# Tying each indirect DMA of two expert layers to a preceding matmul, and dealing the DMAs out in another rhythm

## The chip, the cores and the metric

The kernel runs on one NeuronCore of one Trainium2 chip. The metric is the device time of one execution in microseconds, and the time of a version is the median of several executions. Five engines run side by side, each in its own program order: TensorE (PE in the profile; its weight loads are shown apart as PEld), VectorE (DVE), ScalarE (ACT), GpSimd (POOL) and SyncE (SP, which here only issues DMAs). They wait for one another through semaphores.

## The reference

The program is a chain of eight blocks on an activation `x` of 8 sequences by 512 tokens by 128 channels, all in float32. What follows is cut to the order of the blocks and to the expert layer, which the change concerns.

```python
x = x + circulant_ssm(layernorm(x))       # "rotate" block
x = x + ffn(layernorm(x))                 # "lora" block
x = x + encoder(layernorm(x))             # 4 layers of linear attention
x = x + ffn(layernorm(x))
x = x + rotary_attention(layernorm(x))    # "attended" steps
x = x + experts(layernorm(x))             # expert layer m
x = x + gated_linear_attention(layernorm(x))   # "gated" steps
x = x + experts(layernorm(x))             # expert layer n, then the output

def experts(x):                           # 8 experts, the best 2 for each token
    xn = rms_norm(x, norm_scale)
    scores = einsum('bsd,ed->bse', xn, w_router)
    ids = top_k(scores, 2)[1]
    c = take_along_axis(softmax(scores), ids, -1)
    val, gate = split(einsum('bsd,ehd->bseh', xn, w_up), 2, -1)   # hidden size 352
    y = einsum('bseh,edh->bsed', val * silu(gate), w_down)
    return x + sum(take_along_axis(y, ids[..., None], 2) * c[..., None], 2)
```

## The kernel before, in words

**Experts by sorting.** Class `Experts` does one expert layer, here called m (the first) and n (the second). Its sequences are cut into groups: m has two groups of 4 sequences, n has three groups of 2, 4 and 2. For one group the work goes like this.

1. `choose` (VectorE, with four small matmuls) finds the two best experts of each token and, from counts, a slot for each (token, expert) pair, so that slots of one expert lie in whole tiles of 128. It is a generator of twelve steps, and the last one fills the list `todo`.
2. `posts` issues the indirect DMAs on POOL's queue. A **row** (line 1122, `slots<-xn,rpos`) scatters 128 tokens to their slots in DRAM. There are 2 for every 128 tokens, that is 32 rows for a group of 4 sequences and 16 for a group of 2.
3. `tiles` is a generator that does one expert tile of 128 slots in each turn. `fetch` reads four tiles of slots back (line 1168, `xr<-slots`, on SP's queue); it waits for **all** rows of the group. `turned` transposes them (line 1179). Then each tile has two matmuls of width 352 (lines 1235 and 1236), ACT's tanh (1241), two VectorE operations (1248 and 1249), three transposes (1199), a copy by ACT (1201), six matmuls (1208) and ACT's copy to `yr` (1211). A group of 4 sequences has 39 tiles, a group of 2 has 23. The steps are pipelined over turns: a turn does the first matmuls of tile i, the transposes of i-1 and the last matmuls of i-2.
4. For each finished tile, `posts` issues a **given** (line 1133, `given<-yr,to`): an indirect DMA that scatters 128 results to where their tokens are.
5. `combine` reads the results back (line 1267, after all givens of the group) and adds them to `x` (line 1285).

`posts` is a generator as well. Each call of `next` issues at most one DMA: a row if `todo` has one and fewer than 5 finished tiles are waiting, else a given. If nothing is ready it does nothing.

**Order.** The context manager `in_program_order` makes each of PE, DVE, ACT and POOL run its instructions in the order in which the Python code emits them, with one freedom (rows of one group among themselves). So the time at which a DMA can be issued depends on what stands before it in POOL's order, among which are the rsqrt operations that the norms need (line 165 for `ln_rs` and `g_rs`, 966 for `m_rs`, 1663 for `g_rn`). The places of all this are set by hand:

- In `attended_and_experts`, `pipeline` runs the attention's steps for the 8 sequences. Near its end the side stream `first` is called once after every step: `choose` of m's group one, then its rows. Whatever is left of `first` runs after it.
- Then `blend` deals three streams over 42 turns: the tiles of m's group one, `choose` of group two, and `posts`.
- In `gated_and_experts`, `pipeline` runs the gated steps for 4 pairs of sequences, with a side stream `dealt` that has numbered places: `at(now, i)` is place i of round `now`, and each round has 29 places. `before` is layer m, `posts` its remaining DMAs, `own` the DMAs of layer n, and `tiles` the turns of layer n. The gated steps fall in rounds -1 to 4; round 5 holds only tiles, DMAs and `choose`.
- A second `blend` deals the turns of layer n that are left, with `own` and with `combine` of its first two groups. What is left of `own` and the last group's `combine` follow.

Of the kernel before, what the change touches and what calls it, by code (L numbers as in the profile page):

```python
# [912 lines left out]
class Experts:  # L913
# [24 lines left out]
    def apart(self, rows, made):  # L938
# [7 lines left out]
        self.loose[made.ins.name] = group  # L946
        rows.append(made.ins)

    def steps(self, b):

        k, nc = self.k, self.k.nc
# [158 lines left out]
        self.todo.extend((g, t, i) for t in range(g.n) for i in range(2))  # L1110
        yield

    def posts(self, many, upto=0):

        nc = self.k.nc
        while many and not (upto and all(len(g.back) == g.tiles for g in self.groups[:upto])):
            given = [g for g in self.groups if g.ready]
            if self.todo and sum(len(g.ready) for g in given) < 5:  # L1120
                g, t, i = self.todo.pop(0)
                made = nc.gpsimd.indirect_dma_start(  # L1122
                    out=g.slots,
                    out_offset=bass.IndirectOffsetOnAxis(ap=g.pos[:, i, t : t + 1], axis=0),
                    in_=g.xn[:, t, :],
                    in_offset=None,
                )
                self.apart(g.rows, made)
                many -= 1
            elif given:  # L1130
                g = given[0]
                yr, to = g.ready.pop(0)
                made = nc.gpsimd.indirect_dma_start(  # L1133
                    out=g.given,
                    out_offset=bass.IndirectOffsetOnAxis(ap=to, axis=0),
                    in_=yr,
                    in_offset=None,
                )
                self.apart(g.back, made)
                many -= 1  # L1140
            yield

# [149 lines left out]
def chain(*streams):  # L1292
    for one in streams:
        yield from one
# [4 lines left out]
        pass  # L1299


def slow(stream, idle):

    for _ in stream:
        for _ in range(idle + 1):
            yield


def fast(stream, many):

    while True:
        for _ in range(many):
            if next(stream, stream) is stream:
                return
        yield


def idle(many):
    yield from range(many)
# [54 lines left out]
def attended_and_experts(k, o, slots, keep, work, banks, close):  # L1374

    tc = k.tc
    with tc.tile_pool(name="moe1", bufs=1, side="right") as room:
        m = Experts(k, "m", slots, keep, room)  # L1380
        one, two = m.groups
        with tc.tile_pool(name="cau2", bufs=2) as pool, k.banks(**banks["after"]):
            after = attended_steps(k, o, pool)

            def steps(b):
                yield from after(b)
                yield from m.steps(b)

            with in_program_order(tc, m.loose):
                first = chain(m.choose(one), slow(m.posts(2 * one.n), 1))  # L1390


                pipeline(
                    steps,
                    B,
                    (0, 1, -1, 2, 3, -2, 1, -1, 0, 3, 2, 0, 3, 4),
                    side=first,
                    every=1,
                    first=one.seqs + 4,
                )  # L1400
                run(first)
        close()
        m.p3 = work()
        m.hidden()
        with k.banks(**banks["experts"]), in_program_order(tc, m.loose):
            n = turns(one)
            posts = m.posts(2 * two.n + one.tiles + two.tiles)
            blend((m.tiles(one), n), (fast(m.choose(two), 2), n), (chain(idle(3), take(fast(posts, 2), n - 3)), n))
    return m, posts


def gated_and_experts(k, before, posts, slots, keep, banks, out):
# [3 lines left out]
    with tc.tile_pool(name="moe1", bufs=1, side="right") as room:  # L1416
# [5 lines left out]
        with tc.tile_pool(name="gla1", bufs=1) as alone, tc.tile_pool(name="gla", bufs=2) as pool:  # L1422
            with k.banks(**banks["gated"]):
# [15 lines left out]
                def at(now, *places):  # L1439
                    return [(now + 1) * len(ages) + i for i in places]  # L1440

                side = dealt(
                    (before.tiles(last), at(-1, *range(16), *range(17, 28, 2)) + at(0, *range(0, 29, 2)) + at(1, *range(5))),
                    (posts, at(-1, *range(29)) + at(0, *range(29)) + at(1, *range(6))),
                    (whole(posts), at(1, 6)),
                    (before.combine(first), at(-1, *range(6, 15))),
                    (before.combine(last), at(1, *range(8, 15), 17, 19)),
                    (m.choose(one), at(2, *range(19, 29)) + at(3, *range(3))),
                    (own, at(3, *range(3, 29)) + at(4, *range(29)) + at(5, *range(32))),
                    (own, at(5, *range(16, 32))),  # L1450
                    (tiles, at(3, *range(20, 29, 2)) + at(4, *range(0, 29, 4)) + at(5, *range(0, 30, 6))),
                    (m.choose(two), at(4, *range(19, 29)) + at(5, *range(3))),
                    (m.choose(three), at(5, *range(19, 32))),
                )
                with in_program_order(tc, before.loose, m.loose):
                    pipeline(steps, B // 2, ages, side=side, every=1)
                    run(side)
        with k.banks(**banks["experts"]), in_program_order(tc, m.loose):
            left = pieces - 18

            def combined(g):
                yield from until(lambda: len(g.back) == g.tiles)
                yield from idle(3)
                yield from m.combine(g)

            blend((tiles, left), (take(fast(own, 2), left), left), (chain(*(combined(g) for g in m.groups[:2])), left))
            run(own)
            run(m.combine(three))

# [864 lines left out]
```

## Time and profile before

| what | value |
|---|---|
| median of 3 runs | 2083.75 us (2075.97 to 2087.93) |
| profiled execution | 2091.69 us; span from its first to its last instruction 2090.0 us |
| busy, share of the span: PE, PEld, DVE, ACT, POOL | 83%, 57%, 60%, 45%, 35% |
| mean granted TensorE clock | 0.888 |
| rows issued | 128, of 974 ns each on POOL |
| givens issued | 163, of 968 ns each on POOL |
| DMA on POOL's queue | 20.47 MB, 2.9% of 16 engines' span |

In the profile, busy time is what an engine spends in its own instructions; issuing a DMA from SP isn't counted. "Idle before" is an engine's idle time ahead of an instruction, and the name after the arrow is what ended it: another engine's instruction, a DMA, "issue" when the profile shows no wait that ended just then, or "remote" when the semaphore was updated at that moment but no instruction of the profile ended close to it. The end of a matmul is computed by the profiler, not observed.

### The profile page before, as it was taken

Reading aid. Unit: us, or ns where it says so; the run is one execution under the profiler, and the core shown is the slowest. Engines: PE = TensorE matmul, PEld = TensorE weight load, DVE = VectorE, ACT = ScalarE, POOL = GpSimd, SP = SyncE. Lnnn points to the kernel's source line nnn. Section 1 sums busy time; section 2 is a strip of 40 time slices with the busy share of each in tenths; the row PEclk is TensorE's granted clock in tenths of the full one; section 3 lists DMA queues with packets and bytes.
Section 4 is the critical chain, followed back from the end, with each engine's and each line's share of the span. In section 5 each row is a group of like instructions: output and inputs, shape, how many; then the busy total and the mean of one; then the engine's idle time right before and its main releaser. Section 6 shows DMA issues by size and latency. Waiting matters only on the chain. (4 is left out here: it accounts for less than half of the span.)

```text
span 2090.0 us, 29883 instructions
## 1 busy us (share of the span) xinstructions
PE 1742.2 (83%) x10171; PEld 1189.5 (57%) x10171; DVE 1249.7 (60%) x4147; ACT 950.9 (45%) x1747; POOL 730.3 (35%) x866
## 2 busy tenths in 40 slices
PE   4998789999998698999988727898898886726995
PEld 2655567888776455444346515665565565614774
DVE  6654788888877654555546624456657844613554
ACT  1022556666654322666665413454545443403553
POOL 2111333333334421454454365522121114355342
PEclk9888899999998789999988858998999876857998
DMA  9600000000000200000000011221001001112232
GB/s 273 107 1 1 0 1 1 1 1 1 1 1 1 109 23 41 1 2 2 2 1 1 5 58 53 65 62 47 16 11 39 12 1 41 30 49 71 68 102 63
DMA packets 79390, 71.25 MB, mean 34 GB/s; under 512 B 6560, under 2 KB 73120, under 8 KB 78336
## 3 DMA queue, kind: packets, MB, share of 16 engines
q1 hardware_dynamic: 69120, 47.89, 8.9%
q0 software_dynamic: 9536, 20.47, 2.9%
q8 instruction: 86, 1.41, 0.3%
q10 hardware_dynamic: 576, 0.90, 0.1%
q14 instruction: 72, 0.59, 0.1%
HBM read 34.98 MB, written 34.25 MB: 33 GB/s over the span
## 5 line engine op out<-in xcount | busy, mean ns | idle before, releaser
L165 POOL TENSOR_TENSOR ln_rs<-rs_v,mhalf 128x4 f32<-128x4 f32 x144 | 150.9, 1049 | 427.3 <-DVE rs_v L164 412.8
L1133 POOL DMA_INDIRECT given<-yr,to x163 | 157.9, 968 | 339.5 <-ACT yr L1211 288.7
L1248 DVE SCALAR_TENSOR_TENSOR half<-half,ps_a 128x352 f32<-128x352 f32 x163 | 84.6, 519 | 243.5 <-ACT half L1241 205.9
L672 ACT ACTIVATE pr<-ps_s 128x1024 f32<-128x1024 f32 x160 | 155.1, 1021 | 64.6 <-PE ps_s L662 64.3
L1236 PE MATMUL ps_a<-w_m,xt 128*128 x326 | 136.0, 501 | 55.7 <-DVE half L1248 23.6
L1122 POOL DMA_INDIRECT slots<-xn,rpos x128 | 124.6, 974 | 61.5 <-issue 45.7
L676 POOL TENSOR_SCALAR_AFFINE_SELECT pr<-pr 128x256 f32<-128x256 f32 x256 | 101.4, 418 | 112.2 <-ACT pr L672 109.1
L1235 PE MATMUL ps_a<-w_m,xt 128*128 x326 | 135.7, 500 | 5.7 <-ACT xt L1181 4.1
L1201 ACT COPY gt<-ps_b 128x384 f32<-128x384 f32 x163 | 77.9, 478 | 131.3 <-PE ps_b L1199 99.4
L530 PEld LDWEIGHTS ps_c<-w_e,mlp_g 128*128 128x128 f32 x1024 | 126.6, 198 | 15.1 <-issue 14.8
L530 PE MATMUL ps_c<-w_e,mlp_g 128*128 128x128 f32 x1024 | 128.8, 281 | 0.1
L522 PE MATMUL ps_a<-zt,w_e 128*128 128x512 f32 x256 | 123.7, 607 | 0.9 <-ACT zt L211 0.9
L1236 PEld LDWEIGHTS ps_a<-w_m,xt 128*128 128x128 f32 x326 | 63.6, 203 | 104.7 <-DVE half L1248 33.8
L1241 ACT ACTIVATE half<-ps_a 128x352 f32<-128x352 f32 x163 | 75.5, 463 | 86.4 <-PE ps_a L1235 69.4
L178 DVE BATCH_NORM_AGGREGATE ln_mv<-ln_st 128x2 f32<-128x6 f32 x576 | 99.9, 178 | 16.0
L1199 PEld LDWEIGHTS ps_b<-w_ident,hid 128*128 128x128 f32 x489 | 64.7, 149 | 74.3 <-issue 34.6
L1199 PE MATMUL ps_b<-w_ident,hid 128*128 128x128 f32 x489 | 86.9, 289 | 20.2 <-DVE hid L1249 15.0
L1249 DVE SCALAR_TENSOR_TENSOR hid<-half,ps_a 128x352 f32<-128x352 f32 x163 | 85.0, 521 | 29.3 <-remote 7.5
L523 ACT ACTIVATE mlp_g<-ps_a,w_col 128x512 f32<-128x512 f32 x128 | 85.6, 686 | 35.4 <-PE ps_a L522 35.4
L224 POOL TENSOR_TENSOR xe<-xe,w_erow 128x512 f32<-128x512 f32 x64 | 82.2, 1304 | 55.2 <-DVE ks L480 52.8
L373 ACT ACTIVATE mlp_g<-ps_a,w_col 128x512 f32<-128x512 f32 x64 | 44.0, 687 | 125.5 <-PE ps_a L372 124.8
L662 PE MATMUL ps_s<-qm,rot 32*128 32x128 f32 (+3 forms) x1024 | 98.6, 472 | 2.1 <-ACT pr L672 2.1
(362 smaller groups left out, 4010.8 us busy)
## 6 DMA issues: line engine op xcount, KB each, us to landing
xr<-slots SPq DMA_DIRECT2D x37, 260.0 KB
y<-given SPq DMA_DIRECT2D x32, 256.0 KB
slots<-blank SPq DMA_DIRECT2D x3, 2535.0 KB
w_m<-in_m_dram SPq DMA_DIRECT2D x2, 2244.0 KB
w_e<-in_e_dram SPq DMA_DIRECT2D x2, 1700.0 KB
slots<-blank SPq DMA_DIRECT2D x2, 1495.0 KB
given<-yr,to POOLq DMA_INDIRECT x163
x<-in_u_dram SPq DMA_DIRECT2D x8, 256.0 KB
```

The source lines that it names most:

```text
L165: nc.gpsimd.tensor_tensor(out, v, self.mhalf[:, :n], ALU.pow)
L178: nc.vector.bn_aggr(mv[:, t, :], st[:, t, :])
L522: nc.tensor.matmul(ph, w1[:, c * P : (c + 1) * P], ht, start=True, stop=True)
L530: nc.tensor.matmul(py[:, t, :], g[:, c, t * P : (t + 1) * P], w2[:, c, :], start=(c == 0), stop=(c == 3))
L662: nc.tensor.matmul(halves[g // 2][:, g % 2, at : at + S - u * P], kr[rows, u * P : (u + 1) * P], qm[rows, i, u * P : S], start=True, stop= ...
L672: nc.scalar.activation(pr, sc, AF.Exp)
L676: nc.gpsimd.affine_select(out=v, in_=v, pattern=[[0, 2], [1, P]], compare_op=ALU.is_ge, fill=0.0, base=0, channel_multiplier=-1,)
L1122: made = nc.gpsimd.indirect_dma_start(out=g.slots, out_offset=bass.IndirectOffsetOnAxis(ap=g.pos[:, i, t : t + 1], axis=0), in_=g.xn[:, t, :],
L1133: made = nc.gpsimd.indirect_dma_start(out=g.given, out_offset=bass.IndirectOffsetOnAxis(ap=to, axis=0), in_=yr, in_offset=None,)
L1199: nc.tensor.transpose(pt[:, q, :], hid[:, q, :], k.ident)
L1235: nc.tensor.matmul(pg, xt, w["experts"][:, bass.ds(o + HID, HID)], start=True, stop=True)
L1236: nc.tensor.matmul(pv, xt, w["experts"][:, bass.ds(o, HID)], start=True, stop=True)
```

## The change

A method `behind` is added. After each indirect DMA is made, it looks back through the instructions emitted so far in the block, finds the last one of PE, and makes the DMA wait for it. The schedules by hand are changed as well: rows of m's group one come at every step instead of every second one; in the first `blend` the choice runs at three steps a turn and the DMAs at 2, 2 and 1, with what is left of group two's rows issued right after; in the gated rounds m's second group starts later, and n's DMAs, tiles and choice of group two are placed differently; in the last `blend` the DMAs come at 1 and 2 a turn instead of 2. The number of DMAs and all arithmetic stay as they were.

```diff
--- before.py
+++ after.py
@@ -946,6 +946,13 @@
         self.loose[made.ins.name] = group
         rows.append(made.ins)
 
+    def behind(self, made):
+        tc = self.k.tc
+        for i in reversed(tc.nc.cur_bb.bb.instructions):
+            if i.engine == mybir.EngineType.PE:
+                tc.add_manual_dep(made.ins, i.name, SYNC, reason="not all of them at once")
+                return
+
     def steps(self, b):
 
         k, nc = self.k, self.k.nc
@@ -1110,12 +1117,12 @@
         self.todo.extend((g, t, i) for t in range(g.n) for i in range(2))
         yield
 
-    def posts(self, many, upto=0):
+    def posts(self, many):
 
 
 
         nc = self.k.nc
-        while many and not (upto and all(len(g.back) == g.tiles for g in self.groups[:upto])):
+        while many:
             given = [g for g in self.groups if g.ready]
             if self.todo and sum(len(g.ready) for g in given) < 5:
                 g, t, i = self.todo.pop(0)
@@ -1126,6 +1133,7 @@
                     in_offset=None,
                 )
                 self.apart(g.rows, made)
+                self.behind(made)
                 many -= 1
             elif given:
                 g = given[0]
@@ -1137,6 +1145,7 @@
                     in_offset=None,
                 )
                 self.apart(g.back, made)
+                self.behind(made)
                 many -= 1
             yield
 
@@ -1299,20 +1308,14 @@
         pass
 
 
-def slow(stream, idle):
-
-    for _ in stream:
-        for _ in range(idle + 1):
-            yield
-
-
-def fast(stream, many):
+def fast(stream, *many):
 
     while True:
-        for _ in range(many):
-            if next(stream, stream) is stream:
-                return
-        yield
+        for n in many:
+            for _ in range(n):
+                if next(stream, stream) is stream:
+                    return
+            yield
 
 
 def idle(many):
@@ -1387,7 +1390,7 @@
                 yield from m.steps(b)
 
             with in_program_order(tc, m.loose):
-                first = chain(m.choose(one), slow(m.posts(2 * one.n), 1))
+                first = chain(m.choose(one), m.posts(2 * one.n))
 
 
                 pipeline(
@@ -1405,7 +1408,9 @@
         with k.banks(**banks["experts"]), in_program_order(tc, m.loose):
             n = turns(one)
             posts = m.posts(2 * two.n + one.tiles + two.tiles)
-            blend((m.tiles(one), n), (fast(m.choose(two), 2), n), (chain(idle(3), take(fast(posts, 2), n - 3)), n))
+            blend((m.tiles(one), n), (fast(m.choose(two), 3), n), (chain(idle(4), take(fast(posts, 2, 2, 1), n - 4)), n))
+            while len(two.rows) < 2 * two.n:
+                next(posts)
     return m, posts
 
 
@@ -1440,30 +1445,31 @@
                     return [(now + 1) * len(ages) + i for i in places]
 
                 side = dealt(
-                    (before.tiles(last), at(-1, *range(16), *range(17, 28, 2)) + at(0, *range(0, 29, 2)) + at(1, *range(5))),
+                    (before.tiles(last), at(-1, 4, *range(7, 29)) + at(0, *range(0, 29, 2)) + at(1, *range(4))),
                     (posts, at(-1, *range(29)) + at(0, *range(29)) + at(1, *range(6))),
+                    (posts, at(-1, *range(9))),
                     (whole(posts), at(1, 6)),
-                    (before.combine(first), at(-1, *range(6, 15))),
+                    (before.combine(first), at(-1, *range(9, 18))),
                     (before.combine(last), at(1, *range(8, 15), 17, 19)),
                     (m.choose(one), at(2, *range(19, 29)) + at(3, *range(3))),
                     (own, at(3, *range(3, 29)) + at(4, *range(29)) + at(5, *range(32))),
-                    (own, at(5, *range(16, 32))),
-                    (tiles, at(3, *range(20, 29, 2)) + at(4, *range(0, 29, 4)) + at(5, *range(0, 30, 6))),
-                    (m.choose(two), at(4, *range(19, 29)) + at(5, *range(3))),
+                    (own, at(5, *range(0, 32, 2))),
+                    (tiles, at(3, *range(20, 29, 2)) + at(4, *range(0, 29, 4)) + at(5, *range(0, 32, 4))),
+                    (fast(m.choose(two), 2), at(4, *range(19, 26))),
                     (m.choose(three), at(5, *range(19, 32))),
                 )
                 with in_program_order(tc, before.loose, m.loose):
                     pipeline(steps, B // 2, ages, side=side, every=1)
                     run(side)
         with k.banks(**banks["experts"]), in_program_order(tc, m.loose):
-            left = pieces - 18
+            left = pieces - 21
 
             def combined(g):
                 yield from until(lambda: len(g.back) == g.tiles)
                 yield from idle(3)
                 yield from m.combine(g)
 
-            blend((tiles, left), (take(fast(own, 2), left), left), (chain(*(combined(g) for g in m.groups[:2])), left))
+            blend((tiles, left), (take(fast(own, 1, 2), left), left), (chain(*(combined(g) for g in m.groups[:2])), left))
             run(own)
             run(m.combine(three))
 
```

## The prediction

> **What bounds the kernel now.** I first read the table by stage, PE against time, because the whole-span share (83% busy) mixes stages. Columns: stretch, length, busy time with instruction counts for PE, PEld, DVE, ACT and POOL, granted clock, DMA share, GB/s.
>
> ```profile
> core 0: us, PE busy (x) PEld busy (x) DVE busy (x) ACT busy (x) POOL busy (x), PEclk, DMA share, GB/s
> 1246.50:1355.00 108.50, 85.88 (x429) 60.90 (x430) 46.05 (x139) 40.87 (x104) 57.57 (x60) 0.86 0.20 60
> ...
> 1821.00:1915.00 94.00, 37.46 (x150) 26.32 (x150) 22.94 (x86) 14.05 (x36) 55.15 (x58) 0.63 0.16 49
> 1915.00:2071.00 156.00, 149.30 (x886) 114.99 (x885) 86.99 (x239) 85.56 (x206) 61.55 (x66) 0.99 0.27 80
> ```
>
> In the last stretch expert tiles run alone and PE is full: PE is the bound. Between 1821 and 1915 no compute engine is above 40%, and POOL is busiest, with indirect DMAs. Next I read the timelines of that dip, engine by engine: start, duration, instruction, and in brackets the idle time before it and its releaser.
>
> ```profile
> 1847.15 0.95 POOL L1122 DMA_INDIRECT slots<-xn,rpos  x1 [0.31 <-issue]
> 1848.41 0.96 POOL L1122 DMA_INDIRECT slots<-xn,rpos  x1 [0.30 <-issue]
> 1849.67 0.95 POOL L1122 DMA_INDIRECT slots<-xn,rpos  x1 [0.30 <-issue]
> ```
> ```profile
> 1843.26 1.54 PE L1236 MATMUL ps_a<-w_m,xt 128*128 x2 [6.68 <-issue]
> 1847.76 0.88 PE L1199 MATMUL ps_b<-w_ident,hid 128*128 128x128 f32 x3 [2.96 <-DVE hid L1249]
> 1869.17 1.65 PE L1208 MATMUL ps_a<-w_m,gt 128*128 x6 [20.53 <-ACT yr L1211]
> ```
> ```profile
> 1856.26 0.48 ACT L1201 COPY gt<-ps_b 128x384 f32<-128x384 f32 x1 [13.62 <-remote]
> 1868.85 0.27 ACT L1211 COPY yr<-ps_a 128x128 f32<-128x128 f32 x1 [12.11 <-remote]
> ```
>
> POOL issues a DMA every 1.26 us. The three transposes end at 1848.64, yet ACT's copy of them starts at 1856.26: 7.6 us late. It waits for PE's semaphore, whose update appears in the trace at 1856.19; four more updates of PE come within 0.2 us of one another, at 1868.8, after the burst has stopped. The work is done, and the message is late. So I counted, over the whole trace, PE instructions whose semaphore shows no update within 1 us of their end, by how many indirect DMAs POOL had just issued back to back (under 1.45 us apart): none, 1 of 1677; one, 3 of 312; two or three, 14 of 69; four to six, 26 of 58; seven or more, 15 of 17. **Runs of indirect DMAs delay other engines' semaphores**, and the delay begins at the third or so.
>
> The cost per stage comes from the starts of line 1235. A tile turn takes 2.19 us undisturbed, and 2.31 on average over n's group two (1919.6 to 2007.4, 38 gaps). m's group one takes 3.21 (1248.4 to 1370.4), and 2.87 in the part with one row and one given a turn (1285.2 to 1348.3, 22 gaps). In n's group one, one gap alone is 39.3 (1835.8 to 1875.1). Last, the waits of PE: before m's first tile it waits for the rows,
>
> ```profile
> PE ps_b L1179 <- DMA xr<-slots: 27.4, 2, 26.6
> ```
>
> and POOL's rows fill 1202.95 to 1241.97 there, broken only by one pair of rsqrts.
>
> **What the Trainium skill says.** "DMA: Bandwidth & Descriptors", section on SWDGE, HWDGE and iDMA: for a DMA issued from GpSimd its cores compute the descriptors and write them to rings in SBUF. The trace agrees that each occupies POOL, 0.96 us; that page says nothing of other engines' semaphores. "Perfetto Trace Analysis", section on the TensorE instruction: a matmul's end is estimated from its size, and the semaphore update comes after PSUM has acknowledged and must then propagate. That allows a gap; that 1676 of 1677 are under 1 us without a burst shows that 7.6 isn't the estimate's error. "TensorE: Matmul & The Clock Gate", section on what is happening: PE's clock falls to half after an idle window of about 3.4 us. The trace agrees: 0.50 in 1850 to 1880. A stall is thus paid for twice. The same page, section on the per-tile semaphore tail, prices an increment at 26.3 ns.
>
> **The change, part by part.** I count DMAs turn by turn from the streams.
>
> 1. *Waits.* 291 DMAs get one. Most of the matmuls named already signal; if all needed another increment, 291 x 26.3 ns = 7.7 us, an estimate from that page, spread over PE and mostly inside other engines' latency: 0 taken, 0 to 8 kept. On POOL a separate wait instruction exists before (at 1853.23), and the spacing there stays 1.26: 0. Queued behind a waiting DMA on POOL are the rsqrts; for them wait DVE's norms, then PE's transposes. Usually the rsqrt needs DVE results that need a later matmul than the one waited for. I take 0; the rival below has the other bound.
>
> 2. *Rows of m's group one.* POOL-bound: 32 x 1.26 = 40 us after `choose` ends at 1189. Before, POOL idled 5.8 us (1193.6 to 1199.4) for lack of rows in its order; doubling their rate fills that. But 14 rather than 7 rows now precede the last `m_rs` (8.8 us later), which the tail can bear, since PE waits for the rows anyway until 1246. The first row starts 2 to 3 us later, since it waits for transposes that end at 1192.3. Taken -4 (-10 to +5).
>
> 3. *m's group one, 5 DMAs in 3 turns instead of 6.* 5 x 1.26 = 6.3 us against 3 x 2.31 = 6.9: POOL gets a pause every third turn, so runs end at about five; before, POOL needed 2.52 a turn and could never catch up. I take 2.6 us a turn, between 2.31 and 2.87, and 5 for the start: 38 x 2.6 + 5 = 104 against 122.0. Taken -18 (-33 to 0).
>
> 4. *Transition.* Rows now end 2 givens and 3 rows after the last turn: 5 x 1.26, then 2.4 to land and 2.9 for `xr` (both in the chain at 1767 and 1769) = 11.6 us. Covered by the gated steps that now stand before the first tile of group two, which took PE and its partners about 10 (1374.7 to 1378.8 and 1386.2 to 1389.2, with evictions between). Taken +2; without that cover +10.
>
> 5. *Gated rounds.* Row runs (9 from 1747.0) are broken up, a few us to gain; waits on POOL, a few to lose. Taken 0 (-8 to +15).
>
> 6. *n's group two.* Choosing two steps at once brings the first row from 1820.65 to about 1818 (its VectorE chain begins at 1807.2). From there to the end of the rounds stand 43 DMAs = 54 us on POOL, for 9 tiles of PE (20 us). So POOL lags, its waits are satisfied already, and runs form again. The difference: a late update now also stops POOL when it reaches the DMA tied to it, and the messages get through. I allow three such pauses of 3 us: 1818 + 54 + 9 = 1881. Then five turns and a fetch before n's group two, 2.2 each with some lead of PE already gained: 1890 against 1919.6. Rows aren't in the way: the 35th DMA holds the last one, 1818 + 44 + 2.4 + 2.9 = 1867. Taken -29 (-50 to -5).
>
> 7. *Last tiles.* 16 rows of group three move into group two's turns, which were free of rows: +2. One given is left after the last turn instead of none: +1.
>
> Sum: -4 - 18 + 2 + 0 - 29 + 2 + 1 = **-46 us**. The profiled execution took 2091.69 (span 2090.0), 8 above the median 2083.75; taken from the median, 2038.
>
> **Rivals.** *Runs stay runs (2066).* Where no matmul stands between posts (the flush, the first places of round -1, three of four places in round 5), all DMAs wait for the same finished matmul, and nothing is spaced. For it: part 6 itself, POOL being 34 us behind PE. Then part 6 gives what the earlier start and three more tiles in the rounds give, about -10, part 3 about -6, part 2 -4: with +2 for the rest, -18. Against it: PE now holds POOL.
>
> *Waits hold up the rsqrts (2108, slower).* Between 1375 and 1807 POOL runs 26 of them:
>
> ```profile
> L966 POOL TENSOR_TENSOR m_rs<-m_v,mhalf 128x8 f32<-128x8 f32 x8 | 13.3, 1659 | 38.7 <-DVE m_v L965 38.7
> L165 POOL TENSOR_TENSOR g_rs<-rs_v,mhalf 128x4 f32<-128x4 f32 x8 | 9.2, 1146 | 62.8 <-DVE rs_v L164 31.5 <-DVE ln_nm L188 18.4 <-DVE rt L1028 12.9
> L1663 POOL TENSOR_TENSOR g_rn<-g_nn,mhalf 128x8 f32<-128x8 f32 x4 | 6.6, 1650 | 12.3 <-DVE g_nn L1662 12.3
> L165 POOL TENSOR_TENSOR ln_rs<-rs_v,mhalf 128x4 f32<-128x4 f32 x6 | 6.5, 1080 | 39.5 <-DVE rs_v L164 39.5
> ```
>
> A DMA that waits for the present turn's matmul (up to 2.2 us) and then takes 1.26 holds one up by 3.5. For 20 of them on PE's path that is 70 us, less the 46: 2084 + 24 = 2108. It decides from 14 of 26 on. For it: POOL is in order, and before it waited only for DVE. Against: in that stretch PE waits only 7.5 us before line 991, the transposes that follow an `m_rs`, and most rsqrts are a step or more ahead of their use.
>
> *Bursts cost almost nothing any more (2000):* both dips close to the bounds of parts 3 and 6.
>
> **How the numbers follow.** Forecast 0.60, runs stay 0.20, slower rival 0.11, full gain 0.09. The range 1998 to 2080 takes in the first, second and fourth with their bounds, and leaves out the third and part of the second's upper end. A measurement tells about 0.5% (10.4 us) from no change: faster means below 2073. Of "runs stay", a quarter lies above that. Faster 0.81, same 0.09, slower 0.10.
>
> **What would show it.** In the profile after: no wait on "remote" over 5 us; line 1235 at about 2.6 us a turn in m's group one; no gap near 39 in n's group one; n's group two starting near 1890 less the earlier gains; POOL's DMAs released by PE matmuls; wait for the first `xr` near 22. Wrong if runs over eight DMAs remain with updates over 4 us late, or if PE's waits after the rsqrts grow by tens of us.

## The result, and the profile after

| kernel | median | ratio to the kernel before, 95% interval |
|---|---|---|
| before | 2084.02 us (2075.97 to 2087.93) | |
| changed | 2055.55 us (2052.61 to 2060.78) | 0.9871 [0.9835, 0.9907] |

The change saves 28.5 us by the medians, and 39.1 between the two profiled executions (2091.69 and 2052.61). One thing has to be known to read all that follows: the kernel before took about 2083 us in two sets of runs and about 2035 in three others, every time in all of its executions, so the first two are called disturbed here and the other three quiet, and ratios are taken within a set. Both traces of this section are from a disturbed one. In a quiet set the changed kernel was run only with forty extra DMAs, which cost nothing measurable where they were tried without the waits; it then takes 2028.01 us, 0.9966 of the kernel before. So most of the gain of this table is a gain in disturbed sets.

By stage, from the starts of the tiles' first matmul (line 1235 before, 1244 after). The second pair of traces is of the same two kernels in another disturbed set, where the medians are 24.8 us apart and the two traced executions 19.0. The differences are those of the unrounded times:

| stretch | predicted | first pair | second pair |
|---|---|---|---|
| up to m's first tile | -4 | 1248.4 to 1241.6: -6.8 | -0.2 |
| m's group one, 38 turns | -18 | 122.0 to 102.6: -19.4 | 122.8 to 103.1: -19.8 |
| its last tile to the first of group two | +2 | 9.9 to 33.4: **+23.5** | 9.8 to 33.6: +23.8 |
| from there to n's first tile | 0 | 394.1 to 383.1: -11.0 | -1.5 |
| n's group one to group two | -29 | 145.2 to 116.8: -28.4 | 140.3 to 116.7: -23.6 |
| from there to the end | +3 | 170.4 to 173.4: +3.0 | +2.3 |
| sum | -46 | -39.1 | -19.0 |

The same stretches in the table by stage of the changed kernel (columns as before: stretch, length, busy time with instruction counts for PE, PEld, DVE, ACT and POOL, granted clock, DMA share, GB/s):

```profile
core 0: us, PE busy (x) PEld busy (x) DVE busy (x) ACT busy (x) POOL busy (x), PEclk, DMA share, GB/s
1241.00:1344.00 103.00, 91.94 (x517) 67.19 (x518) 50.79 (x144) 46.80 (x121) 53.56 (x56) 0.98 0.18 54
1344.00:1378.00 34.00, 15.71 (x60) 9.17 (x60) 11.68 (x25) 13.40 (x24) 14.50 (x16) 0.70 0.32 93
...
1820.00:1880.00 60.00, 31.46 (x129) 21.27 (x127) 18.70 (x71) 12.54 (x33) 37.55 (x40) 0.72 0.20 62
1880.00:2046.00 166.00, 144.06 (x859) 110.16 (x857) 90.09 (x249) 81.25 (x200) 73.18 (x77) 0.96 0.30 87
```

The first row is the gain: PE busy for 92 of 103 us. The second is new: 34 us with PE busy for less than half. The third is what is left of the old dip. POOL's timeline there, beside ACT's and PE's:

```profile
1842.13 0.96 POOL L1129 DMA_INDIRECT slots<-xn,rpos  x1 [0.30 <-issue]
1843.40 0.96 POOL L1129 DMA_INDIRECT slots<-xn,rpos  x1 [0.30 <-issue]
1849.22 0.95 POOL L1141 DMA_INDIRECT given<-yr,to  x1 [4.86 <-ACT half L1250]
```
```profile
1832.96 0.27 ACT L1220 COPY yr<-ps_a 128x128 f32<-128x128 f32 x1 [7.24 <-remote]
```
```profile
1819.52 0.83 PE L1217 MATMUL ps_a<-w_m,gt 128*128 x6
...
1833.28 1.54 PE L1244 MATMUL ps_a<-w_m,xt 128*128 x2 [6.57 <-issue]
```

The run is still there: 24 DMAs back to back from 1814.4. Both engines keep their order and do one such product and one copy for each tile, so the two can be paired: the copy that starts at 1832.96 is that of the product which PE finished at 1820.35, and ACT had been free for 7.24 us. Later comes one of the pauses that step 6 had allowed for, 4.86 us. Last, what PE waits for from m's rows on (total, times, longest):

```profile
PE ps_b L1188 <- DMA xr<-slots: 17.1, 2, 13.9
PE ps_b L1567 <- DVE u L195: 10.4, 1, 10.4
```

The wait for the first `xr` is down from 26.6 to 13.9 (about 22 was expected). The second line is the gated steps' first transpose, 10.4 us in one piece. It was not in the prediction.

### The profile page after: what moved, and what is told of

The parts are those of the page before. It is cut to its first block, busy times and chain, and to the rows that moved or that the text cites. A ratio compares the mean times of both kernels' runs of the same rounds, so it can differ in the third digit from the quotient of the medians.

```text
span 2050.9 us, 29936 instructions
## 1 busy us (share of the span) xinstructions
PE 1724.8 (84%) x10171; PEld 1175.4 (57%) x10171; DVE 1251.0 (61%) x4147; ACT 947.4 (46%) x1747; POOL 731.3 (36%) x866
## 5 line engine op out<-in xcount | busy, mean ns | idle before, releaser
L1129 POOL DMA_INDIRECT slots<-xn,rpos x128 | 123.9, 968 | 95.9 <-issue 32.2
L1245 PE MATMUL ps_a<-w_m,xt 128*128 x326 | 132.7, 490 | 25.7 <-DVE half L1257 10.4
L1244 PE MATMUL ps_a<-w_m,xt 128*128 x326 | 135.0, 498 | 19.8 <-issue 9.0
L1245 PEld LDWEIGHTS ps_a<-w_m,xt 128*128 128x128 f32 x326 | 62.2, 200 | 74.3 <-DVE half L1257 19.4
L224 POOL TENSOR_TENSOR xe<-xe,w_erow 128x512 f32<-128x512 f32 x64 | 82.2, 1304 | 55.2 <-DVE ks L480 55.0
L1208 PE MATMUL ps_b<-w_ident,hid 128*128 128x128 f32 x489 | 84.6, 284 | 15.6 <-DVE hid L1258 11.2
```

The costliest lines, as they stand in the source:

```text
L1129: made = nc.gpsimd.indirect_dma_start(out=g.slots, out_offset=bass.IndirectOffsetOnAxis(ap=g.pos[:, i, t : t + 1], axis=0), in_=g.xn[:, t, :],
L1208: nc.tensor.transpose(pt[:, q, :], hid[:, q, :], k.ident)
L1244: nc.tensor.matmul(pg, xt, w["experts"][:, bass.ds(o + HID, HID)], start=True, stop=True)
L1245: nc.tensor.matmul(pv, xt, w["experts"][:, bass.ds(o, HID)], start=True, stop=True)
```

## The new gap between m's groups

The timeline of the transition shows whom that transpose waits for:

```profile
1358.61 0.95 POOL L1129 DMA_INDIRECT slots<-xn,rpos  x1 [0.30 <-issue]
1361.07 0.88 ACT L191 ACTIVATE u<-x,ln_nm,ln_rs 128x128 f32<-128x128 f32 x2 [10.07 <-DMA slots<-xn,rpos]
...
1361.21 0.60 DVE L195 TENSOR_SCALAR u<-x,ln_mv,ln_rs 128x128 f32<-128x128 f32 x2 [9.77 <-DMA slots<-xn,rpos]
...
1361.65 1.09 PE L1567 MATMUL ps_b<-w_ident,u 128*128 128x128 f32 x4 [10.42 <-DVE u L195]
```

The first row printed is the last row of group two. Both engines' write of `u` is released by this row's DMA, which reads m's `xn`. So the gated norm, it seems, writes `u` where the rows have their source, and waits until the last row has been read. PE then has the gated convolution's inputs, ACT and VectorE work through them for 12 us, and only then comes the tile at 1377.58.

The same wait can be read in the trace of the kernel before. There the last row is issued at 1345.99, inside group one, and the norm stands among the tiles:

```profile
1348.65 0.60 DVE L195 TENSOR_SCALAR u<-x,ln_mv,ln_rs 128x128 f32<-128x128 f32 x2 [2.69 <-DMA slots<-xn,rpos]
```

So the wait isn't new; it was small (2.7 us, and 3.8 in the second pair) and counted in group one. The two stages belong together: from m's first tile to the first tile of group two it is 131.9 us before and 136.0 after, 132.7 and 136.7 in the second pair. Together they lose 4 us, where 16 were to be gained. Two runs move the last row.

**Two DMAs in every turn.**

```diff
-... (chain(idle(4), take(fast(posts, 2, 2, 1), n - 4)), n))
+... (chain(idle(4), take(fast(posts, 2), n - 4)), n))
```

> The changed kernel, but with 2 DMAs in every turn of m's group one (rather than 2, 2, 1), so that by the count of turns the last row of group two is issued in turn 32 of 42 and not after the last. Theory (what the transition lost was the wait of the gated norms for the last row, whose source they overwrite): PE's wait of 10.4 us before line 1567 falls under 3 us, and the stretch from m's last tile of group one to the first of group two from 33.4 to about 24; m's group one itself loses 0 to 5 us, total 2044 to 2051. Rival: 2 DMAs of 1.26 us in a turn of 2.7 leave POOL no slack, runs come back and m's group one goes to 112 or more, total 2055 to 2065.

Measured, in a quiet set: 0.9911 [0.9896, 0.9927]. The transition takes 19.3 us and PE's wait before line 1567 is gone, but group one takes 102.0 us where other changed kernels with waits take 92.6 in quiet sets. The timeline says that it isn't runs:

```profile
1328.60 0.96 POOL L1129 DMA_INDIRECT slots<-xn,rpos  x1 [0.30 <-issue]
...
1330.96 0.60 DVE L195 TENSOR_SCALAR u<-x,ln_mv,ln_rs 128x128 f32<-128x128 f32 x2 [7.67 <-DMA slots<-xn,rpos]
...
1333.24 1.54 PE L1245 MATMUL ps_a<-w_m,xt 128*128 x2 [7.27 <-DVE half L1257]
```

The last row comes earlier, but in this kernel the norm stands earlier in VectorE's order as well, ahead of the last tiles. It waits 7.67 us for the same row, and the tiles' `half` waits behind it. The gap has moved into group one, with the wait that makes it. That turn takes 11.9 us where it takes 2.5 in the other kernels, which is all of the 9.4 us. The theory holds as to the cause, but its 0 to 5 us for group one were too few; the rival's loss of 9 us in that stage came true, for another reason than it gave.

**Rows before givens, with the earlier choice.** The second edit is that of the run with the earlier choice (below).

```diff
+    most = 5
-            if self.todo and sum(len(g.ready) for g in given) < 5:
+            if self.todo and sum(len(g.ready) for g in given) < self.most:
...
+            m.most = 10
```

> The changed kernel with the choice of n's group two a round earlier (as in the run with the earlier choice), and in m's group one up to 10 finished tiles may wait while rows of group two are left (rather than 5), so that rows come before givens. Theory: the last row of group two comes 5 DMAs = 6.3 us sooner, the transition goes from 32 to 34 us to 26 to 28, and with the earlier choice the ratio to the kernel before is 0.978 to 0.982 on a chip without late updates (0.9844 with the earlier choice alone), 0.975 to 0.985 on one with. Rival: the givens that were put off fall into the first gated round and hold up its rsqrts, so that the round loses what the transition gains: 0.984 to 0.987.

Measured, quiet: 1998.10 us, 0.9814 [0.9800, 0.9829]. Group one stays at 92.6, the transition is 22.2 (31.8 with the earlier choice alone), the gated rounds are unchanged (388.3 and 388.0). PE's waits in 1300 to 1400:

```profile
PE ps_b L1209 <- DVE hid L1259: 5.9, 3, 3.0
PE ps_b L1189 <- ACT low L1596: 3.9, 1, 3.9
```

PE's wait for `u` that had 10.4 us in the changed kernel is gone; VectorE's norm still waits 2.2 us for the last row. That row is issued at the start of the last turn instead of 12.6 us after it, which is ten DMAs and not the five that were counted, so the transition fell below the 26 to 28 us of the theory. The rival is refuted. This is the best of all kernels run, and beats the kernel before by 1.9% and the changed one, too; in a disturbed set it was not run.

## What the waits do, and what the places do

**Places alone.** Both calls of `behind` are left out of `posts`.

```diff
-                self.behind(made)
```

> The changed schedule without any of the 291 waits. Theory (the waits break up runs of indirect DMAs): POOL has slack in m's group one by the count alone (5 DMAs of 1.26 us in 3 turns of 2.7), so that stage stays near 103 us, but n's rows of group two run together again: from the first tile of n's group one to that of group two 135 to 145 us rather than 116.8; total near 2075. Rival (the waits do nothing, the places do it all): every stage within 3 us of the changed kernel, total 2055 within 6.

Measured: 2015.14 us, 0.9898 [0.9881, 0.9914]. This set was quiet: the kernel before took 2037.1. Group one takes 92.9 us, the transition 25.9, n's group one to two 95.9.

**Waits alone.** The kernel before, with `behind` and its two calls.

> The old schedule with the 291 waits. Theory: n's dip shrinks (first tile of n's group one to that of group two 145.2 to about 125), and m's group one, where POOL was asked for 2.52 us of DMAs a turn, comes down from 122 to 108 to 115; the transition keeps its 10 us, so total 2050 to 2065. Rival (places do it all): 2084 within 6. Rival (waits hold up the rsqrts between the DMAs): over 2094.

Measured, in the same set: 2032.26 us, 0.9976 [0.9969, 0.9984]; 102.6, 9.5 and 98.5 us. With the old places the waits give 5 us there, and the new places alone give 22. In m's group one the old places owe 8.5 us to a single turn of 10.7 us, in which VectorE's norm waits 7.5 us for the last row; from the eighth turn on the others take 2.2 to 2.6 us with either places. No expectation fits as it was written, since each assumed the late updates of the first traces, and here there was not one. The count of PE updates more than 1 us behind the matmul's end, over all runs of DMAs, is 0 of about 2140 in each of the traces of this set, against 59 in the kernel before's first trace. So I ran both kernels again.

> The kernel before, unchanged, for a trace that stands on the same chip as the next three. In the four kernels run so far on another chip than the first two traces, no PE update at all was late (0 of about 2140 each), and the kernel before took 2037.1 us there. Theory (late updates belong to some chips, and where they occur they follow runs of DMAs): either total 2075 to 2090 with late updates as in the first trace, or total near 2037 with none and m's group one at 105 to 112 us; nothing between. Rival (they come and go by chance from run to run): late updates, but in other places than in the first trace.

> The changed kernel, unchanged, beside the kernel before on the same chip. Theory: if the trace shows late updates, the ratio is 0.987 as at first; if it shows none, what is left is the schedule's gain: 0.988 to 0.992, m's group one near 93 us, transition 32, first tile of n's group one to that of group two 96. Rival (the waits' gain is only that late updates are answered): with none late the waits cost a few us, 0.992 to 0.996.

This set was disturbed: 2075.93 us for the traced execution of the kernel before (its median there is 2082.27) and 2057.50, 0.988 [0.986, 0.990], for the changed one, with late updates in both, in the same stages as at first. The two-valued theory holds. I then tried twice more to have the places alone in a disturbed set.

> The changed schedule without the 291 waits, a second time: the first time it ran on a chip whose traces show no late update at all. Theory on a chip with late updates (waits break up runs, or at least answer late updates): runs come back in m's group one and in n's group two, the first at 108 to 118 us rather than 103, the second (first tile of n's group one to that of group two) at 130 to 145 rather than 117; ratio to the kernel before 0.995 to 1.005 where the changed kernel has 0.988. Rival (places do it all, waits nothing): 0.988 within 0.003 with the changed kernel's stages. On a chip without late updates: 0.990 as before.

> The changed schedule without the 291 waits, and with the twenty extra DMAs of the run before (ten back to back from about 139 us, ten 2.4 us apart from about 163 us), so that one trace answers both questions if it comes from a chip with late updates. Theory there: late updates of PE and ACT in 142 to 151 and none in 163 to 188; and without waits m's group one takes 106 to 118 us and the stretch from the first tile of n's group one to that of group two 125 to 145, where the changed kernel had 103.1 and 116.7, ratio 0.992 to 1.003. Rival (places do it all): both stages within 3 us of the changed kernel's and the transition 6 us shorter (as without waits on the chips with none late), ratio 0.985 to 0.989 and 2 to 8 us more for the extra DMAs. On a chip without late updates: none late anywhere, ratio 0.990 to 0.994, that is the schedule alone and the extra DMAs.

Measured: 2014.85 us, 0.9897 [0.9880, 0.9913], and 2015.13 us, 0.9896 [0.9878, 0.9913]. Both sets were quiet again, the second on a chip with the same number as the disturbed one's, so the difference is not simply tied to that number. What the waits do in a disturbed set is therefore **not settled**. What they do in a quiet one is, by the next run, which is the changed kernel with the extra DMAs that the last run has as well. There are twenty, in a block that the program runs twice, so forty:

> The changed kernel with twice 10 extra indirect DMAs in the feed-forward block, for which nothing waits, this time tied to their places on POOL: ten back to back from about 139 us, and ten from about 163 us with a power of 128x4 after each, so that these start 2.4 us apart. Theory (the run does it): on a chip with late updates, PE and ACT updates over 1 us late from about 142 to 151 and none in 163 to 188. Rival (each DMA delays what is under way, however far apart): late ones in both. Rival (late updates need the other traffic of the expert stages): none in either. On a chip without late updates: none in either. Total 0 to 8 us over the changed kernel's.

Measured, quiet: 2028.01 us, 0.9966 [0.9955, 0.9977]. Without waits the extra DMAs cost nothing that can be measured (2015.13 with them, 2014.85 and 2015.14 without). So with the new places the waits cost **13 us**, where with the old ones they gave 5. The table by stage shows part of it, m's group one with waits and then (last row of the two fences) without:

```profile
1247.00:1340.00 93.00, 88.83 (x519) 68.77 (x520) 51.25 (x144) 50.16 (x121) 53.84 (x57) 0.97 0.21 60
1340.00:1372.00 32.00, 15.41 (x58) 8.98 (x57) 11.72 (x25) 13.37 (x23) 14.22 (x15) 0.72 0.34 99
```
```profile
1244.00:1337.00 93.00, 89.99 (x516) 69.83 (x517) 51.24 (x143) 50.16 (x121) 61.43 (x64) 0.95 0.22 65
1337.00:1363.00 26.00, 15.10 (x62) 10.02 (x61) 11.93 (x25) 13.48 (x24) 6.74 (x7) 0.79 0.36 101
```

In the same 93 us POOL does 64 instructions without waits and 57 with them. Seven DMAs of 1.26 us, 8.8 us of POOL's queue, are left over for the transition, in which POOL has 15 instructions to do rather than 7 and which takes 32 us rather than 26. The first row of m's group one also comes later. VectorE's last write of the choice and POOL's first row, with waits and then without:

```profile
1191.83 0.18 DVE L1126 COPY xn<-rm 128x16 f32<-128x16 f32 x1
...
1195.33 1.04 POOL L1166 DMA_INDIRECT slots<-xn,rpos  x1 [5.90 <-PE ps_b L1035]
```
```profile
1190.87 0.17 DVE L1126 COPY xn<-rm 128x16 f32<-128x16 f32 x1
...
1191.33 1.04 POOL L1166 DMA_INDIRECT slots<-xn,rpos  x1 [2.86 <-DVE xn L1126]
```

The row is 3.0 us later against the choice, but little of it reaches m's first tile: from the end of that write to the tile it is 55.2 or 55.3 us in all four traces of kernels with these places and waits in quiet sets, and 54.3 to 54.6 in the three without waits. That is 0.7 us, and with the 6 us of the transition about half of the 13 is placed. The first tile itself starts anywhere between 1241.5 and 1247.3 with waits and between 1243.4 and 1245.3 without, by what lies ahead of the choice, and the gated rounds take 385.2 against 381.0, 385.4 and 380.5. The rest of the 13 us can't be placed within such differences.

**The choice a round earlier.**

```diff
-                    (fast(m.choose(two), 2), at(4, *range(19, 26))),
+                    (fast(m.choose(two), 2), at(3, *range(19, 26))),
```

> The changed kernel, but with the choice for n's group two one round earlier (right after the choice for group one), so that its 32 rows are dealt over round 4 and not in round 5. Theory (what is left of the dip, PE busy 31.4 of the 60 us after 1820, comes from rows run together in round 5): from the first tile of n's group one to that of group two goes from 116.8 to 100 or less, or the gated round before it grows by at most 5; total 2035 to 2045. Rival: round 4 then has 27 DMAs = 34 us of POOL, and the rsqrts of the last gated pair wait behind them: that round grows by 15 us or more, and the total is 2055 or above.

Measured, quiet: 2005.05 us, 0.9844 [0.9828, 0.9860]. From n's first tile to group two it takes 78.9 us (96.3 in the changed kernel with its extra DMAs), and the gated rounds 388.0 (385.2). So even without any late update the rows of group two set the start of its tiles: 32 rows in round 5 are 40 us of POOL, and PE waits 11.2 us for their `xr` in the changed kernel with its extra DMAs. Spread over round 4 they are covered, that wait is gone, and in place of the rival's loss of 15 us stand 2.8, no more than the rounds differ by anyway.

## Are late updates made by runs of DMAs?

A late record need not be a late consumer, so the consumers themselves were measured: in the tiles, the starts of ACT's three operations, of VectorE's first and of PE's transposes. Each engine does these once for each of the 163 tiles and in one order, so every start can be paired with the end of its own producer, and is compared with the later of that end and the own engine's previous end. Counted are those that start over 1 us late, by how many DMAs POOL had issued back to back when they could have started, and, over all, the sum of what exceeds 0.3 us:

| kernel, set | late, with at most 2 DMAs back to back | with 3 to 6 | with 7 or more | sum |
|---|---|---|---|---|
| before, disturbed | 2 of 715; 0 of 702 | 13 of 81; 18 of 90 | 6 of 19; 8 of 23 | 80.8; 92.7 us |
| changed, disturbed | 0 of 649; 0 of 657 | 18 of 151; 22 of 144 | 5 of 15; 4 of 14 | 61.2; 61.0 us |
| places alone, quiet | 0 of 481 | 0 of 34 | 0 of 300 | 0.1 us |
| changed with extra DMAs, quiet | 0 of 542 | 0 of 122 | 0 of 151 | 0.1 us |

The changed kernel has as many late starts as the kernel before (23 and 26 against 21 and 26); they are shorter. The longest of all is in the second trace of the kernel before, where ACT had been idle for 14.3 us and PE had finished the transposes at 1825.09, PE first:

```profile
1824.22 0.87 PE L1199 MATMUL ps_b<-w_ident,hid 128*128 128x128 f32 x3 [0.85 <-issue]
```
```profile
1853.11 0.48 ACT L1201 COPY gt<-ps_b 128x384 f32<-128x384 f32 x1 [14.29 <-remote]
```

In a quiet set a run does no harm. Here is one of 84 DMAs in the run with places alone, POOL and then ACT:

```profile
1805.64 0.96 POOL L1129 DMA_INDIRECT slots<-xn,rpos  x1 [0.30 <-issue]
1806.91 0.96 POOL L1129 DMA_INDIRECT slots<-xn,rpos  x1 [0.30 <-issue]
1808.17 0.96 POOL L1129 DMA_INDIRECT slots<-xn,rpos  x1 [0.30 <-DMA slots<-xn,rpos]
```
```profile
1805.45 0.48 ACT L1208 COPY gt<-ps_b 128x384 f32<-128x384 f32 x1 [0.51 <-PE ps_b L1206]
...
1807.64 0.48 ACT L1208 COPY gt<-ps_b 128x384 f32<-128x384 f32 x1 [0.51 <-PE ps_b L1206]
```

The copies come every 2.19 us, each released by PE with no delay. POOL's spacing is the same 1.26 us as in the disturbed traces. In these traces runs are thus needed for long delays, but don't suffice: something that differs from set to set must be there, too. By the medians the disturbed sets cost the kernel before 47 us (2082.3 less 2035) and the changed one 29.5 (2057.5 less 2028.0), 17.5 less; the consumers' delays fall from 86.8 to 61.1 us on average, 25.7 less. The delays are thus large enough and move the right way, but they are not an account of the time: they come to about twice what is lost.

Two runs put a run of DMAs where none was, in the feed-forward block (the second was to be the control with gaps). `go` issues twelve indirect DMAs of 128 rows, each to a DRAM tile of its own, and the block is run twice:

```diff
+            if b == B - 1:
+                go()
```

> The changed kernel, and besides 12 indirect DMAs of 128 rows, for which nothing waits, one behind the other on POOL in the feed-forward block at about 163 us, where POOL has nothing to do for 33 us and PE is full. Theory (runs hold back the other engines' semaphore updates): on a chip with late updates, ACT's activations there wait on remote updates for 2 to 10 us each, PE loses 5 to 15 us in 163 to 185, and the total is 5 to 15 us over the changed kernel's; on a chip without, 0 to 2 us. Rival (late updates come from what else the expert stages do, the fetches on SP's queue or the traffic in DRAM): 0 to 2 us on either.

> The same 12 DMAs in the same place, with an operation of POOL of about 1.05 us (a power of 128x4) after each, so that they start some 2.4 us apart instead of 1.26. Theory (it is the run, not the DMA): no update of PE over 1 us late in 163 to 196, total 0 to 2 us over the changed kernel's. Rival (each DMA costs the same wherever it stands): PE loses as much as with the run.

Both were in the disturbed set: 2067.24 us, 0.9923 [0.9901, 0.9945], and 2087.71 us, 1.0027 [1.0017, 1.0036], where the changed kernel took 2057.50. In neither did the operations stand where they were meant to, since nothing tied them to their place in the source. The twelve DMAs of the first pass began at 96.88 and at 116.03, eleven of them back to back in both (1.26 to 1.40 us apart), ahead of norms. In the second the powers stood in one block ahead of other rsqrts:

```profile
17.46 26.28 POOL L335 TENSOR_TENSOR b_rest<-all,mhalf 128x4 f32<-128x4 f32 x24
43.71 1.01 POOL L165 TENSOR_TENSOR ln_rs<-rs_v,mhalf 128x4 f32<-128x4 f32 x1
```

The totals are therefore no price of a late update. The second has no gaps and is no control; it took 20 us more than the first, with 26 us of POOL ahead of rsqrts. What the traces do show: between 90 and 125 us the changed kernel's trace holds all 78 updates of PE, ACT and VectorE, the first run's 78 of 90, and the second's, between 110 and 145 us, 73 of 86. Yet ACT's activations started on time. Here they are with the run of DMAs and, from the changed kernel in the same set, without:

```profile
103.57 0.69 ACT L402 ACTIVATE mlp_g<-ps_a,w_col 128x512 f32<-128x512 f32 x1 [8.93 <-issue]
105.27 0.69 ACT L402 ACTIVATE mlp_g<-ps_a,w_col 128x512 f32<-128x512 f32 x1 [1.02 <-issue]
```
```profile
103.04 0.69 ACT L373 ACTIVATE mlp_g<-ps_a,w_col 128x512 f32<-128x512 f32 x1 [8.93 <-PE ps_a L372]
104.75 0.69 ACT L373 ACTIVATE mlp_g<-ps_a,w_col 128x512 f32<-128x512 f32 x1 [1.02 <-PE ps_a L372]
```

PE's matmuls for them ended at 103.53, 105.24, 106.94 and 107.96. The next update of PE that the trace holds comes at 108.93, 0.01 us after the end of another matmul, whose own it is, so the four records are not late but missing; "issue" stands where the profile found none. The traces of disturbed sets lack such records elsewhere too: those of the kernel before have 2079 and 2076 updates of PE for 2134 instructions, those of quiet sets have all. A count of updates therefore mixes late ones with missing ones, and only the consumers tell them apart. That a run makes consumers late outside the expert stages is not shown: four activations are too few to exclude it. The runs with DMAs tied to their places (ten back to back, and ten that came out 2.31 us apart) fell into quiet sets, and had none late in either place, so the comparison of run and gaps stays open.

## Why the prediction was right or wrong

The total was 2038 forecast and 2055.6 measured, 17.5 us too low, and one step carries the miss. That both sets of the comparison were disturbed is luck: the delays from which the forecast was worked out aren't there in a quiet set, where the change, with the extra DMAs, gives 0.9966, less than what the prediction took as no change.

1. *Waits, 0.* Wrong in quiet sets, where with the new places they cost 13 us against a bound of 8, and not measured by themselves in a disturbed one. The working counted semaphore increments, priced at 26.3 ns each by the Trainium skill's page "TensorE: Matmul & The Clock Gate" (section on the per-tile semaphore tail). No run here measures that price. Most of the half that could be placed came from POOL's queue, which loses 8.8 us in a stage in which its DMAs fill nearly all the time.
2. *Rows of m's group one, -4.* -6.8 and -0.2, within the bounds given. The part that the change can have is steadier than that: from the choice's last write to m's first tile 59.1 us before and 56.2 after, 59.1 and 56.4 in the second pair, -2.9 and -2.8. The first row came 3.0 us later for its wait, as foreseen.
3. *m's group one, -18.* -19.4 and -19.8; 102.6 us against 104. The number was right, the reason in part. Late starts are hardly fewer in this stage (9 and 10 against 11 and 12), but their sum falls from 26.4 and 29.5 us to 17.2 and 18.3. POOL, which at 2.52 us of DMAs a turn was said never to catch up, doesn't slow the turns by itself: with two DMAs a turn and no late update they take 2.2 us. And in a quiet set, where this stage takes 102.6 with the old places and 92.6 with the new ones, 8.5 of the difference is the norm's wait for the last row, which has gone to the next stage.
4. *Transition, +2.* **This step failed: +23.5.** The gated rounds that follow are 11 us shorter in the first pair, but only 1.5 in the second. The working took the cost of the last rows as 11.6 us, and covered them by the gated steps that stand before the first tile. But these steps start with a norm that writes over the rows' source and so wait for the rows themselves. The cover was behind what it was to cover, and the gated work that stands first came on top. The overlap was wrong, and with it the total of steps 3 and 4, which lose 4 us together. When the last row comes earlier, the wait goes (22.2 us) or moves with the norm.
5. *Gated rounds, 0.* -11.0 and -1.5, the first outside the bounds of -8 to +15. If gated work done ahead of m's second group were the reason, the second pair, with the same transition, should show it too, and doesn't; it stays open.
6. *n's group two, -29.* -28.4 and -23.6. The run of 24, a long pause of 4.86 us after it and shorter ones of 1.0 to 2.1 us came much as in the working, and n's group two starts at 1877.5, where 1890 less the earlier gains is 1876. The gain seems to be nearly all delay: in quiet sets the old places with waits take 98.5 us and the new places 95.9 (the kernel before itself has no trace there), and the late starts of this stage sum to 54.4 and 63.2 us before and to 33.1 and 32.2 after. Whether the waits or the places shorten them is not shown, since neither was run alone in a disturbed set.
7. *Last tiles, +3.* +3.0 and +2.3.

The slower rival, rsqrts behind waiting DMAs, did not come. POOL's groups of instructions in the gated rounds (busy, mean ns, then idle before and its releaser):

```profile
L973 POOL TENSOR_TENSOR m_rs<-m_v,mhalf 128x8 f32<-128x8 f32 x8 | 13.4, 1683 | 29.4 <-DVE m_v L972 29.4
L165 POOL TENSOR_TENSOR g_rs<-rs_v,mhalf 128x4 f32<-128x4 f32 x8 | 9.2, 1145 | 52.4 <-DVE rs_v L164 26.0 <-DVE ln_nm L188 13.2 <-DVE rt L1035 13.1
L1669 POOL TENSOR_TENSOR g_rn<-g_nn,mhalf 128x8 f32<-128x8 f32 x4 | 6.6, 1651 | 6.2 <-DVE g_nn L1668 6.2
```

The rsqrts still wait for VectorE, not VectorE for them; POOL arrives a little later than before (29.4 us of waiting for 38.7) and that is all. Of the signs that were named, two came out as in "runs stay runs": there are waits on remote over 5 us, and a run of 24 DMAs remains with a copy 7.2 us late, which was to mean that the prediction is wrong. (Step 6 itself had let such runs form again, so sign and step disagreed.) The total, 2055.6, is also nearer to that rival's 2066 than to the forecast of 2038. The stages are not: the rival had about -6 for m's group one and -10 for n's group two, where -19 and -28 or -24 were measured. The lost transition brought the total near the rival's, for another reason than the rival's. The general statement under all of it, that runs of DMAs delay the other engines, holds for the traces it was read from and not for the quiet sets.

One reading behind that statement was off. ACT's copy that starts at 1856.26 is not that of the transposes that end at 1848.64, but of the ones before, which ended at 1834.80; paired in order, the copy of the former comes at 1869.37. The delay is thus longer than the 7.6 us given: ACT had been free for 13.6. And the count by length of a run took missing records for late ones; the starts paired above show the same trend.

## What to carry to other kernels

When a stall is said to be covered by other work, follow that work's own inputs and its output's memory: a buffer that is read by the late transfer makes the cover wait as well. A wait on a queue that is busy for nearly all of a stage isn't free even if it costs nothing where it stands, since the work that it pushes out comes back at the next point where somebody needs the queue's last entry. And before a delay that has no instruction behind it is made the theory, look at the same kernel in another set of runs, and at the start of the consumers, each paired with its own producer, rather than at the records of updates. Where a change moves work across the border of two stages, add the two up before calling one of them a gain.

## What was unexpected of the hardware

The same kernel takes 2035 or 2082 us for a whole set of runs, and what differs between the sets is not known. In the slower sets an operation of ACT started up to 14.3 us after ACT and its input were both ready, while POOL issued long runs of indirect DMAs; in the quiet ones 84 DMAs back to back, at the same spacing of 1.26 us, delay nobody. And the traces of the slower sets lack 55 to 58 of PE's 2134 updates in the kernel before, so that an update which can't be found may be missing from the trace while the engine that waits for it went on 0.04 us after the matmul's end.
